# The start of an LSTM kernel: h0 @ Wh joins the product of x's first pair, the first step's cell is placed among the last operations of Wh's split, and the first pairs of x are waited for one by one

## The chip, the cores and the metric

The kernel runs on one core of one Trainium2 chip. A core has five engines, each of which works through its own queue in order: TensorE (PE; its weight loads are shown apart as PEld), VectorE (DVE), ScalarE (ACT), GpSimd (POOL) and SyncE (SP). They meet through semaphores. The metric is the device time of one execution in microseconds. Before the change three runs gave 2269.09, 2270.43 and 2270.66 us, median 2270.43.

## What is computed

An LSTM over 16 sequences of 512 steps, with 512 inputs and 512 hidden units, whose outputs are added to x:

```python
def ref(x, h0, Wx, Wh, b):            # x (16, 512, 512), h0 (16, 512)
    xW = jnp.einsum('ntd,dg->ntg', x, Wx) + b
    def step(carry, xw_t):
        prev_h, prev_c = carry
        a = xw_t + prev_h @ Wh        # (16, 2048): gates i, f, o, g
        i = sigmoid(a[:, :H]); f = sigmoid(a[:, H:2*H])
        o = sigmoid(a[:, 2*H:3*H]); g = tanh(a[:, 3*H:])
        next_c = f * prev_c + i * g
        next_h = o * tanh(next_c)
        return (next_h, next_c), next_h
    _, hs = lax.scan(step, (h0, zeros), swapaxes(xW, 0, 1))
    return x + swapaxes(hs, 0, 1)
```

Every step needs the h of the step before it; only the products with Wx are free of the recurrence.

## The kernel before, in words

**Layout.** Two steps form a pair of 32 rows (2 times 16 sequences); 8 pairs are loaded as one tile `xs`. Each of the four column groups of TensorE (32 output partitions each) takes one quarter of the hidden units, so a product is always four matmuls side by side. The hidden units are also cut into two halves, called a and b (0 and 1), so that one half's cell can be computed while the other half's products run.

**Products with Wx.** `turn_x(q)` (L173) transposes pair q of x on DVE into `xT`; ahead of it a small copy `seen` (L179) takes one column of each block, so that the wait for the DMAs of x is made once. `project(q, c)` (L185) multiplies quarter c of the inputs into a PSUM bank `xb[q % 4]` that already holds the bias, in fp32, as two matmul records for each matmul. `seed(t, h)` (L196) has ACT copy half h of the gates of step t from that bank to the bank `gates[h][t % 2]`, with the rows of the pair's other step set to zero by a mask.

**Products with Wh.** Wh is scaled and split into three fp16 parts, `wq[0]` to `wq[2]`. The split works on 8 pieces n = 0 to 7 of 128x1024 (quarter c = n // 2 of the rows, half of the gates). For each: q1 rounds the scaled weight to fp16 (L469 on ACT or L471 on DVE), r1 takes the rest (L474, DVE), q2 rounds that (L478, ACT), r2 takes the rest again (L481, DVE), and q3 rounds that (L483, ACT). The scales come from the largest magnitudes of Wh: `bound` (L430) reduces rows on DVE (L436) or on ACT (L434), and `scales(h)` (L444) makes the factors for half h of the rows with seven small DVE operations. `products(t, i, kh, h)` (L204) multiplies the parts of half kh of h by `wq[i-1]` into the gates of half h, eight matmuls each.

**Step 0** has no split h. `first_products` (L219) multiplies h0, transposed on DVE into `hT0` (L501), by Wh itself in fp32, straight into the banks `gates[h][0]`, after the seeds.

**A step's cell** is the list `STEP` (L24), executed by `act` (L270): turn and turno transpose the gates on DVE (L246), fold and foldo combine parts (L253), tanh, sig, sigo and scale are ACT's (L280 to L288), mix and cell DVE's (L290, L296), ctanh ACT's (L298), p1 writes the first fp16 part of the new h (L306), h the fp32 one (L300), copy (L310), p2 (L312), rem (L316) and p2r (L320) the others. Half a's products can start with p1_a; the others need p2, copy and p2r.

**TensorE's order in a step** is the list `STEP_PE` (L23): twelve products, named by part, half of h and half of the gates, and then two quarters (x0, x1) of a product with Wx for a pair that comes two pairs later. The first of a step is q3aa.

**What sets the order.** All five queues are filled in the order in which the program issues (the scheduling is by hand). The start does this: DMAs of Wh, Wx and most of x on SP's queue, of h0 and of the first three pairs of x on POOL's (`load_first`, L156, 8 DMAs a pair); bias into the four xb banks (L418); then a loop over the 8 pieces (L493) that issues the split's operations one piece behind the other. In its third round (n == 2) it issues `turn_x` for three pairs, `hT0`, and the products with Wx for pairs 0 and 1; in its sixth (n == 5) the seeds of steps 0 and 1. After the loop the step loop begins with t = 0: its first products, x0 and x1 for pair 2, and its cell.

DMAs on a queue share a small set of semaphores. An engine waits for each semaphore by itself, so that a copy that needs eight DMAs has several waits ahead of it.

Of the kernel before, what the change touches and what calls it, by code (L numbers as in the profile page):

```python
# [7 lines left out]
FP = mybir.dt.float32  # L8
# [3 lines left out]
ALU = mybir.AluOpType  # L12
PSUM = bass.MemoryType.PSUM

P = 128
Q = 32
XB = 16
LO = 4096.0
# [6 lines left out]
    "turn_a turno_a fold_a tanh_a foldo_a sig_a turn_b sigo_a scale_a mix_a fold_b "  # L25
    "tanh_b cell_a ctanh_a turno_b foldo_b sig_b p1_a sigo_b h_a copy_a mix_b p2_a "
    "scale_b cell_b rem_a ctanh_b p2r_a p1_b h_b copy_b p2_b rem_b p2r_b"
)


@with_exitstack
def lstm_residual(ctx: ExitStack, tc: tile.TileContext, x, h0, wx, wh, b, out):
# [28 lines left out]
    nc = tc.nc  # L61
    N, T, D = x.shape
    H = h0.shape[1]
# [37 lines left out]
    wq = [const.tile([P, NK, G * H], HP, tag=f"wq{i}", name=f"wq{i}") for i in range(3)]  # L101

    wx_j = wx_sb.rearrange("p k (g c j u) -> p k j g c u", g=G, c=NK, j=NJ)
    wh_j = wh_sb.rearrange(
        "p k (e g h c j u) -> p k e h j g c u", e=2, g=2, h=2, c=2, j=NJ
    )
    wq_j = [
        w.rearrange("p k (g h c j u) -> p k h j g c u", g=G, h=2, c=2, j=NJ) for w in wq
    ]
    bias = const.tile([P, G * P], FP, tag="bias", name="bias")  # L110
    mask = const.tile([P, S2], FP, tag="mask", name="mask")
    zero = const.tile([1, G * P], HP, tag="zero", name="zero")
    amax = const.tile([P, 5], FP, tag="amax", name="amax")
    top = const.tile([P, 2], FP, tag="top", name="top")
    bits = const.tile([P, 2, 2], FP, tag="bits", name="bits")
    sc = const.tile([P, 2, 4], FP, tag="sc", name="sc")
# [55 lines left out]

    def turn_x(q):  # L173
        s, i = divmod(q, XP)
        if i == 0 or q == FIRST:

            a, e = (0, FIRST) if q == 0 else (i, XP)
            seen = tmp.tile([P, XP, NK], FP, tag="seen", name=f"seen_{q}")
            nc.vector.tensor_copy(  # L179
                seen[:, a:e], xs[s].rearrange("p i (c u) -> p i c u", c=NK)[:, a:e, :, 0]  # L180
            )
        xT[q] = xtp.tile([P, NK, Q], FP, tag="xT", name=f"xT_{q}")
        nc.vector.transpose(xT[q].rearrange("p c m -> p (c m)"), xs[s][:, i])  # L183

    def project(q, c):  # L185
        for j in range(NJ):
            nc.tensor.matmul(  # L187
                xb[q % NXB][j * Q : (j + 1) * Q],
                lhsT=xT[q][:, c],
                rhs=wx_j[:, c, j],  # L190
                start=False,
                stop=False,
                skip_group_check=True,
            )

    def seed(t, h):  # L196
        nc.scalar.mul(  # L197
            gates[h][t % 2][:, :GU].rearrange("p (g u) -> p g u", g=G),
            xb[t // 2 % NXB].rearrange("p (g h u) -> p h g u", g=G, h=2)[:, h],
            mask[:, t % 2 : t % 2 + 1],  # L200
        )
# [14 lines left out]
                    skip_group_check=True,  # L216
                )

    def first_products(kh, h, hT):  # L219
        for cc in range(2):  # L220
            for e in range(2):
                for j in range(NJ):
                    nc.tensor.matmul(
                        gates[h][0][j * Q : (j + 1) * Q, (1 - e) * P : (2 - e) * P],
                        lhsT=hT[:, 2 * kh + cc],
                        rhs=wh_j[:, 2 * kh + cc, e, h, j],
                        start=False,
                        stop=False,
                        skip_group_check=True,
                    )  # L230


    gc = [state.tile([P, 2, 2 * N], FP, tag=f"gc{h}", name=f"gc{h}_init") for h in range(2)]
# [118 lines left out]
    def residual(p):  # L352
        s, i = divmod(p, XP)
        if i == 0:
            ob[s] = outp.tile([P, XP, P], FP, tag="ob", name=f"ob_{s}")
        hb = work.tile([P, P], FP, tag="hb", name=f"hb_{p}")
        nc.vector.transpose(hb, hs[p].rearrange("p c m -> p (c m)"))  # L357
        add = nc.vector if p == NP - 1 else nc.gpsimd
        add.tensor_tensor(ob[s][:, i], hb, xs[s][:, i], ALU.add)  # L359
        if p == NP - 1:  # L360
            put_pair(s, i, [nc.sync, nc.scalar])
        elif s == NS - 1:
            put_pair(s, i, [nc.sync])
        elif i == XP - 1:
            put(s)
# [8 lines left out]
    for c in range(NK):  # L374
        for e in range(2):
            f = slice(e * GH, (e + 1) * GH)
            nc.sync.dma_start(out=wh_sb[:, c, f], in_=wh[c * P : (c + 1) * P, f])
    nc.vector.memset(zero, 0.0)
    nc.vector.memset(h_in, 0.0)
    nc.vector.memset(ones, 1.0)  # L380
    for j in range(NJ):
# [45 lines left out]
                )  # L427
    nc.scalar.copy(bias, xb[0])

    def bound(i, c, on_act, f=slice(0, G * H)):  # L430
        w = wh_sb[:, c, f]
        if on_act:
            junk = tmp.tile([P, G * H], HP, tag="junk", name=f"junk_{i}", bufs=1)
            nc.scalar.activation(junk[:, f], w, AF.Abs, accum_out=amax[:, i : i + 1])  # L434
        else:
            nc.vector.tensor_reduce(  # L436
                amax[:, i : i + 1],
                w,
                mybir.AxisListType.X,
                ALU.max,  # L440
                apply_absolute_value=True,
            )

    def scales(h):  # L444


        nc.vector.tensor_reduce(
            top[:, h : h + 1], amax[:, 3 * h : 3 + 2 * h], mybir.AxisListType.X, ALU.max
        )
        t = top[:, h : h + 1].bitcast(I32)  # L450
        e, inv = bits[:, h, 0:1], bits[:, h, 1:2]
        nc.vector.tensor_scalar(
            inv.bitcast(I32), t, EXP, EXP, ALU.bitwise_and, ALU.bitwise_xor
        )
        nc.vector.tensor_scalar(e.bitcast(I32), t, EXP, None, ALU.bitwise_and)
        nc.vector.tensor_scalar(RS2[h], inv, 2.0**12, 0.5, ALU.mult, ALU.min)
        nc.vector.tensor_scalar(RS[h], inv, 2.0**13, 1.0, ALU.mult, ALU.min)
        nc.vector.tensor_scalar(S[h], e, 2.0**-14, 1.0, ALU.mult, ALU.max)
        nc.vector.tensor_scalar(RSL[h], RS[h], 1.0 / LO, None, ALU.mult)

    r1, r2 = {}, {}

    def split(n, k):

        c, e = divmod(n, 2)
        w = wh_sb[:, c, e * GH : (e + 1) * GH]
        f = [q[:, c, (1 - e) * GH : (2 - e) * GH] for q in wq]
        if k == 0 and n < 6:
            nc.scalar.mul(f[0], w, RS2[c // 2])  # L469
        elif k == 0:  # L470
            nc.vector.tensor_scalar(f[0], w, RS2[c // 2], None, ALU.mult)  # L471
        elif k == 1:
            r1[n] = tmp.tile([P, GH], FP, tag="r1", name=f"r1_{n}")
            nc.vector.scalar_tensor_tensor(  # L474
                r1[n], w, RS[c // 2], f[0], ALU.mult, ALU.subtract
            )
        elif k == 2:
            nc.scalar.copy(f[1], r1[n])  # L478
        elif k == 3:
            r2[n] = tmp.tile([P, GH], FP, tag="r2", name=f"r2_{n}")  # L480
            nc.vector.tensor_tensor(r2[n], r1[n], f[1], ALU.subtract)  # L481
        else:
            nc.scalar.mul(f[2], r2[n], LO)  # L483

    NH = 2 * NK
    bound(0, 0, False)
    bound(1, 1, True, slice(0, GH))
    bound(2, 1, False, slice(GH, 2 * GH))
    scales(0)
    split(0, 0)  # L490
    split(0, 1)
    split(1, 0)
    for n in range(NH):  # L493
        if n == 1:
            bound(3, 2, False)
            bound(4, 3, True)
            scales(1)
        if n == 2:
            for q in range(FIRST):
                turn_x(q)  # L500
            nc.vector.transpose(hT0.rearrange("p c m -> p (c m)"), h_in)  # L501
            for q in range(2):
                for c in range(NK):
                    project(q, c)
        if n + 1 < NH:
            split(n + 1, 1)
        split(n, 2)
        split(n, 3)
        if n:
            split(n - 1, 4)  # L510
        if n + 2 < NH:
            split(n + 2, 0)
        if n == 5:
            for t in range(2):
                for h in range(2):
                    seed(t, h)
    split(NH - 1, 4)

    for t in range(T):
        s, ti = divmod(t, XB)  # L520
        q, half = divmod(t + 4, 2)
        if ti == 0:
            hist[s] = outp.tile([P, XP, NK, Q], FP, tag="hist", name=f"hist_{s}")

        for op in STEP_PE.split():
            if op[0] == "x":
                if q < NP:
                    project(q, 2 * half + int(op[1:]))
            elif t:
                products(t, int(op[1]), "ab".index(op[2]), "ab".index(op[3]))  # L530
            elif op[1] == "3":
                first_products("ab".index(op[2]), "ab".index(op[3]), hT0)

        for op in STEP.split():
            name, h = op.split("_")
            act(t, name, "ab".index(h))

        if t + 2 < T:
            seed(t + 2, 0)
        if t % 2:  # L540
            for h in range(2):
                unscale(t // 2, h)
            if q + 1 < NP:
                turn_x(q + 1)
        else:
            if t and q + 1 < NP:
                put_bias(q + 1)
            if t:
                residual(t // 2 - 1)
        if t + 2 < T:  # L550
            seed(t + 2, 1)
        if ti == 0 and s + 2 < NS:
            load_xs(s + 2)
# [29 lines left out]
```

## Time and profile before

| | |
|---|---|
| profiled execution, us | 2270.51 |
| its span, first to last instruction, us | 2268.2 |
| median of three runs, us | 2270.43 |
| PE busy | 2234.5 us (99%), 57444 matmul records |
| DVE busy | 1957.2 us (86%) |
| ACT busy | 1839.7 us (81%) |
| products with Wh (L210) | 49056 records, 1427.4 us |
| products with Wx (L187) | 8192 records, 966.7 us |
| first product of step 1 starts (timeline) | 44.78 us |

How to read it: the span runs from the first to the last instruction; the time of the execution has some 2.3 us around that. The mean duration of a matmul record is longer than its share of the engine, since four run side by side. Busy shares over the whole span tell of the 512 steps; the start, some 2% of the span, has to be read in the timeline, in order of time.

### The profile page before, as it was taken

The page shows a single profiled execution, that of the slowest core. Times are in us where ns is not written, and L with a number is a line of the kernel's source. Part 1 is how long each engine was busy: PE and PEld are TensorE (multiplying, and loading weights), DVE is VectorE, ACT ScalarE, POOL GpSimd, SP SyncE. Part 2 cuts the span into 40 slices and gives each one's busy share as a digit, 9 for nine tenths or more (in the row PEclk, how much of TensorE's full clock was granted, in tenths as well). Part 3 has the DMA queues.
Part 4 walks back from the last instruction along what each step waited for, and adds up shares of the span by engine and source line. Part 5 has one row for each costly group of instructions (what it writes and reads, how often), then busy time and mean ns, then how long its engine had stood idle before and what let it go on. Part 6 is the DMA issues. An engine that isn't in the chain of part 4 may idle for free.

```text
span 2268.2 us, 138001 instructions
## 1 busy us (share of the span) xinstructions
PE 2234.5 (99%) x57444; PEld 1466.8 (65%) x57444; DVE 1957.2 (86%) x11853; ACT 1839.7 (81%) x7959; POOL 131.1 (6%) x287
## 2 busy tenths in 40 slices
PE   6999999999999999999999999999999999999997
PEld 3666666666666666666666666666666666666665
DVE  7888888888888888888888888888888888888887
ACT  6888888888888888888888888888888888888887
POOL 2000000000000000000000000000000000000000
PEclk9999999999999999999999999999999999999999
DMA  5011111111111111111111111111111111111001
GB/s 166 16 22 23 16 17 16 22 22 19 17 17 19 22 22 16 17 17 22 23 18 16 17 20 23 22 16 17 16 23 22 19 16 17 20 22 21 15 9 17
DMA packets 297716, 50.93 MB, mean 22 GB/s; under 512 B 294593, under 2 KB 295041, under 8 KB 297089
## 3 DMA queue, kind: packets, MB, share of 16 engines
q1 hardware_dynamic: 295872, 41.85, 11.4%
q8 instruction: 450, 7.37, 1.4%
q14 instruction: 176, 1.44, 0.2%
q0 software_dynamic: 896, 0.23, 0.1%
q10 hardware_dynamic: 322, 0.04, 0.0%
HBM read 25.21 MB, written 16.78 MB: 19 GB/s over the span
## 4 chain that ended last, share of the span: by engine, by line
PE 97%; DMA 1%; DVE 1%; issue 0%; ACT 0%; POOL 0%; SPq 0%; POOLq 0%; DVEq 0%
PE gates L210 59%; PE xb L187 38%; DMA xs<-in_x_dram 1%; DVE r L481 0%; DMA h_in<-in_cond_dram 0%; DVE r L474 0%; ACT wq L483 0%; SPq L347 0%; POOL h_in L382 0%; DMA out_dram<-ob 0%; DVE wq L471 0%; DVE xT L183 0%; POOLq L578 0%; DVE pr L290 0%; POOL ob L359 0%
## 5 line engine op out<-in xcount | busy, mean ns | idle before, releaser
L210 PEld LDWEIGHTS <-parts 128*32 128x32 f16 x49056 | 1224.7, 96 | 442.2 <-DVE parts L306 306.0
L210 PE MATMUL gates<-wq,parts 128*32 128x256 f16 x49056 | 1427.4, 273 | 7.0 <-DVE parts L306 7.0
L187 PE MATMUL xb<-wx_sb,xT 128*32 128x512 f32 x8192 | 966.7, 593 | 17.4 <-DMA xs<-in_x_dram 17.4
L246 DVE STREAM_TRANSPOSE gt<-gates 128x192 f32<-128x192 f32 x1024 | 392.0, 383 | 216.2 <-PE gates L210 168.1
L187 PEld LDWEIGHTS xb<-wx_sb,xT 128*32 128x32 f32 x8192 | 235.4, 110 | 344.1 <-issue 340.3
L197 ACT ACTIVATE gates<-xb,mask 128x256 f32<-128x256 f32 x1024 | 451.3, 441 | 0.0
L280 ACT ACTIVATE gc<-pre 128x32 f32<-128x32 f32 x1022 | 234.6, 230 | 259.7 <-DVE pre L253 248.3
L288 ACT ACTIVATE os<-so,sc 128x32 f32<-128x32 f32 x1024 | 329.6, 322 | 16.7
L310 ACT COPY parts<-parts 128x32 f16<-128x32 f16 x1022 | 214.3, 210 | 132.2 <-DVE parts L306 132.2
L253 DVE SCALAR_TENSOR_TENSOR pre<-gt 128x96 f32<-128x96 f32 x1024 | 255.1, 249 | 0.0
L282 ACT ACTIVATE sif<-pre 128x64 f32<-128x64 f32 x1024 | 244.9, 239 | 0.0
L359 POOL TENSOR_TENSOR ob<-hb,xs 128x128 f32<-128x128 f32 x255 | 116.5, 457 | 2121.6 <-DVE hb L357 2039.4
L246 DVE STREAM_TRANSPOSE gto<-gates 128x64 f32<-128x64 f32 x1024 | 231.2, 226 | 0.0
L286 ACT ACTIVATE so<-preo 128x32 f32<-128x32 f32 x1024 | 227.0, 222 | 0.0
L298 ACT ACTIVATE tch<-gc 128x32 f32<-128x32 f32 x1024 | 226.8, 221 | 0.1
L320 DVE SCALAR_TENSOR_TENSOR parts<-rem,parts 128x32 f16<-128x32 f32 x1022 | 195.9, 192 | 35.5
L253 DVE SCALAR_TENSOR_TENSOR preo<-gto 128x32 f32<-128x32 f32 x1024 | 193.6, 189 | 17.5
L312 DVE SCALAR_TENSOR_TENSOR parts<-parts,hist 128x32 f16<-128x32 f16 x1022 | 193.3, 189 | 17.7
L290 DVE TENSOR_TENSOR pr<-sif,gc 128x64 f32<-128x64 f32 x1022 | 205.8, 201 | 0.0
L306 DVE TENSOR_TENSOR parts<-os,tch 128x32 f16<-128x32 f32 x1022 | 196.9, 193 | 0.0
L296 DVE TENSOR_TENSOR gc<-pr 128x32 f32<-128x32 f32 x1024 | 193.3, 189 | 0.0
L300 DVE SCALAR_TENSOR_TENSOR hist<-os,tch 128x32 f32<-128x32 f32 x1024 | 190.2, 186 | 0.3 <-ACT tch L298 0.3
(49 smaller groups left out, 740.1 us busy)
## 6 DMA issues: line engine op xcount, KB each, us to landing
xs<-in_x_dram SPq DMA_DIRECT2D x992, 16.0 KB, 2.1
out_dram<-ob SPq DMA_DIRECT2D x992, 16.0 KB, 1.6
wh_sb<-in_L_cond_Wh_dram SPq DMA_DIRECT2D x8, 512.0 KB, 7.8
wx_sb<-in_L_cond_Wx_dram SPq DMA_DIRECT2D x8, 512.0 KB, 11.7
out_dram<-ob SPq DMA_DIRECT2D x60, 8.0 KB, 1.5
xs<-in_x_dram SPq DMA_DIRECT2D x32, 10.0 KB, 2.3
xs<-in_x_dram POOLq DMA_DIRECT2D x24, 8.0 KB, 5.2
h_in<-in_cond_dram POOLq DMA_DIRECT2D x4, 8.0 KB, 6.0
```

Of the source, the lines that this page charges most:

```text
L187: nc.tensor.matmul(xb[q % NXB][j * Q : (j + 1) * Q], lhsT=xT[q][:, c], rhs=wx_j[:, c, j], start=False, stop=False, skip_group_check=True,)
L197: nc.scalar.mul(gates[h][t % 2][:, :GU].rearrange("p (g u) -> p g u", g=G), xb[t // 2 % NXB].rearrange("p (g h u) -> p h g u", g=G, h=2)[: ...
L210: nc.tensor.matmul(g[j * Q : (j + 1) * Q, :GU], lhsT=a[:, cc, k * N : (k + 2) * N], rhs=wq_j[i - 1][:, 2 * kh + cc, h, j], start=False, st ...
L246: nc.vector.transpose(gt.rearrange("p b m -> p (b m)"), gates[h][t % 2][:, b0 * Q : b1 * Q])
L253: nc.vector.scalar_tensor_tensor(pre.rearrange("p g (c n) -> p (g c) n", c=2), gt[:, :, (1 - t % 2) * N : (2 - t % 2) * N], 1.0 / LO, gt[: ...
L280: nc.scalar.activation(gc[h][:, 0], v["pre", h][:, 0], AF.Tanh)
L282: nc.scalar.activation(new("sif", t, h, [P, 2, 2 * N]), v["pre", h][:, 1:3], AF.Sigmoid)
L286: nc.scalar.activation(new("so", t, h, [P, 2 * N]), v["preo", h][:, 0], AF.Sigmoid)
L288: nc.scalar.mul(new("os", t, h, [P, 2 * N]), v["so", h], S[h])
L290: nc.vector.tensor_tensor(new("pr", t, h, [P, 2, 2 * N]), v["sif", h], gc[h], ALU.mult)
L298: nc.scalar.activation(new("tch", t, h, [P, 2 * N]), gc[h][:, 1], AF.Tanh)
L310: nc.scalar.copy(slots(t, h, 2), slots(t, h, 0))
```

## The change

All of it lies ahead of step 1; the step loop then runs from t = 1.

- The order of the start is now one written list, `START`, which the function `start` executes. It names every bound (`b.0.v`: quarter 0 on DVE; `.s`: on ACT; `1a`, `1b`: a quarter's two halves), scale (`S.0`), operation of the split (`q1.2.v`: q1 of piece 2 on DVE), pair of x (`xT.0`), product (`H.c`, `P.q.c`), seed and operation of step 0's cell. So pieces are taken in the order 2, 0, 3, 1, 5, 7, 6, 4, five of the roundings are DVE's (q1.0, q1.2, q2.2, q3.3, q3.7; before, q1.6 and q1.7 were), and step 0's cell stands between the last operations of the split.
- `H.c` multiplies quarter c of h0 by Wh into `xb[0]`, ahead of the products with Wx of pair 0. Since h0's rows in `hT0` are those of the pair's first step, the seed carries the sum into step 0's gates. The matmuls have 256 columns instead of 128, and there are half as many. `first_products` into the gates is gone.
- `turn_x` makes its small copy for each of the pairs 0, 1 and 2 by itself.
- `Z` adds twelve matmuls of zeros, one partition deep and 512 columns wide, to the bank `xb[3]`, after the first half of pair 2's product.
- The bounds have eight places (a memset of `amax` is new); r1 has four buffers instead of three. The load of the third `xs` tile is issued at the same place in SP's queue.

```diff
+START = (
+    "b.0.v hT H.0 b.1a.v b.1b.v H.1 S.0 q1.2.v q1.3.s H.2 q1.0.v q1.1.s r1.2 b.2.s r1.0 "
+    "H.3 r1.3 b.3a.s b.3b.s q2.2.v xT.0 q2.3.s r1.1 P.0.0 q2.0.s r2.2 q2.1.s S.1 q3.2.s "
+    "r2.0 P.0.1 q1.5.s r2.3 q3.0.s r2.1 q1.7.s q3.3.v q3.1.s P.0.2 xT.1 q1.6.s r1.5 "
+    "q1.4.s P.0.3 r1.7 P.1.0 seed.0.0 r1.6 seed.0.1 P.1.1 seed.1.0 turn_a turno_a q2.7.s "
+    "turn_b xT.2 fold_a q2.6.s fold_b P.1.2 foldo_a r1.4 tanh_a sig_a sigo_a scale_a "
+    "tanh_b sig_b P.1.3 P.2.0 P.2.1 turno_b r2.6 q2.4.s q2.5.s mix_a mix_b cell_a foldo_b "
+    "Z r2.4 ctanh_a q3.6.s cell_b p1_a h_a q3.4.s r2.5 sigo_b ctanh_b scale_b seed.1.1 "
+    "copy_a p2_a rem_a r2.7 q3.5.s p1_b h_b p2r_a copy_b q3.7.v p2_b rem_b p2r_b seed.2.0 "
+    "seed.2.1"
+)
...
-    wh_j = wh_sb.rearrange(
-        "p k (e g h c j u) -> p k e h j g c u", e=2, g=2, h=2, c=2, j=NJ
-    )
+    wh_j = wh_sb.rearrange("p k (e g c j u) -> p k e j g c u", e=2, g=2, c=NK, j=NJ)
...
-        if i == 0 or q == FIRST:
-            a, e = (0, FIRST) if q == 0 else (i, XP)
+        if i == 0 or q <= FIRST:
+            a, e = (i, i + 1 if q < FIRST else XP)
             seen = tmp.tile([P, XP, NK], FP, tag="seen", name=f"seen_{q}")
...
-    def first_products(kh, h, hT):
-        for cc in range(2):
-            for e in range(2):
-                for j in range(NJ):
-                    nc.tensor.matmul(
-                        gates[h][0][j * Q : (j + 1) * Q, (1 - e) * P : (2 - e) * P],
-                        lhsT=hT[:, 2 * kh + cc],
-                        rhs=wh_j[:, 2 * kh + cc, e, h, j],
...
+    def first_products(c):
+        for e in range(2):
+            for j in range(NJ):
+                nc.tensor.matmul(
+                    xb[0][j * Q : (j + 1) * Q, (1 - e) * GU : (2 - e) * GU],
+                    lhsT=hT0[:, c],
+                    rhs=wh_j[:, c, e, j],
...
-            r1[n] = tmp.tile([P, GH], FP, tag="r1", name=f"r1_{n}")
+            r1[n] = tmp.tile([P, GH], FP, tag="r1", name=f"r1_{n}", bufs=4)
...
+    def start(op, a="", b=""):
+        if op == "b":
+            bound(a, b == "s")
+        elif op == "S":
+            scales(int(a))
+        elif op == "hT":
             nc.vector.transpose(hT0.rearrange("p c m -> p (c m)"), h_in)
...
+        elif op == "xT":
+            turn_x(int(a))
+        elif op == "H":
+            first_products(int(a))
+        elif op == "P":
+            project(int(a), int(b))
+        elif op == "Z":
+            for _ in range(12):
+                zeros(xb[NXB - 1], False)
+        elif op == "seed":
+            seed(int(a), int(b))
+        elif "_" in op:
+            name, h = op.split("_")
+            act(0, name, "ab".index(h))
+        else:
+            split(op, int(a), b == "s")
+
+    hist[0] = outp.tile([P, XP, NK, Q], FP, tag="hist", name="hist_0")
+    for op in START.split():
+        start(*op.split("."))
+    load_xs(2)
+
+    for t in range(1, T):
...
-            elif t:
+            else:
                 products(t, int(op[1]), "ab".index(op[2]), "ab".index(op[3]))
-            elif op[1] == "3":
-                first_products("ab".index(op[2]), "ab".index(op[3]), hT0)
```

## The prediction

> **What bounds the kernel now.** I read the page first, then the timeline of the first 60 us, then the chain of waits there, then busy time in stretches cut where the granted TensorE clock changes.
>
> The page: 511 of the 512 steps are TensorE work.
>
> ```profile
> span 2268.2 us, 138001 instructions
> PE 97%; DMA 1%; DVE 1%; issue 0%; ACT 0%; POOL 0%; SPq 0%; POOLq 0%; DVEq 0%
> PE gates L210 59%; PE xb L187 38%; DMA xs<-in_x_dram 1%; DVE r L481 0%; DMA h_in<-in_cond_dram 0%; DVE r L474 0%; ACT wq L483 0%; SPq L347 0%; POOL h_in L382 0%; DMA out_dram<-ob 0%; DVE wq L471 0%; DVE xT L183 0%; POOLq L578 0%; DVE pr L290 0%; POOL ob L359 0%
> ```
>
> The chain is all TensorE, in the products with Wh's parts (L210) and with Wx (L187). The code of steps 1 to 511 is not edited, and from step 2 on TensorE has no gap (434.00 us busy in 1000 to 1434). So the change is worth what it moves one point: the end of step 1's TensorE work. The timeline of that region (start, duration, engine, line, what, in brackets the idle time before it and what ended it):
>
> ```profile
> 26.96 0.17 DVE L179 COPY seen<-xs 128x12 f32<-128x12 f32 x1 [4.30 <-DMA xs<-in_x_dram]
> ...
> 36.54 3.70 PE L223 MATMUL gates<-wh_sb,hT 128*32 128x128 f32 x128 [0.57 <-ACT gates L197]
> ...
> 42.26 0.38 DVE L246 STREAM_TRANSPOSE gt<-gates 128x192 f32<-128x192 f32 x1
> ...
> 44.53 0.19 DVE L306 TENSOR_TENSOR parts<-os,tch 128x32 f16<-128x32 f32 x1
> ...
> 44.78 4.10 PE L210 MATMUL gates<-wq,parts 128*32 128x256 f16 x96 [2.83 <-DVE parts L306]
> ...
> 48.71 1.89 PE L187 MATMUL xb<-wx_sb,xT 128*32 128x512 f32 x16
> ...
> 50.43 2.79 PE L210 MATMUL gates<-wq,parts 128*32 128x256 f16 x96
> ```
>
> DVE stands still 4.30 us until all three pairs of x have landed, then works without a pause; step 0's cell (from 42.26) waits behind the whole split; TensorE waits for the cell's first product p1 (44.53). Step 1's TensorE work runs to **50.60** (the chain of waits has L210 again from there). Its 96 products take 4.10 us where step 2's take 2.62 (chain), and the stretches say why (columns: stretch, length, busy time of five engines, granted clock, DMA):
>
> ```profile
> 37.24:40.66 3.42, 3.42 (x120) 3.08 (x112) 3.38 (x4) 2.88 (x4) 0.00 (x0) 1.00 0.17 25
> 40.66:44.07 3.41, 1.29 (x13) 0.13 (x4) 3.00 (x10) 3.15 (x7) 0.00 (x0) 1.00 0.16 24
> 44.07:47.48 3.41, 2.70 (x52) 2.10 (x56) 2.12 (x16) 2.31 (x11) 0.00 (x0) 0.50 0.22 33
> 47.48:50.60 3.12, 3.12 (x76) 1.75 (x68) 2.41 (x15) 1.77 (x10) 0.00 (x0) 1.00 0.16 26
> ```
>
> After 3.41 us with TensorE 38% busy the clock is halved; after one with 79% it is whole again. Step 1 pays 4.10 - 2.62 = 1.48 us for it.
>
> **The change, part by part.**
>
> *Waits by pair.* The chain of waits gives when the last DMA of each pair lands: 10.09 + 5.86 = 15.95, 16.23 + 4.97 = 21.20, 21.48 + 5.21 = 26.69. The instruction of `turn_x` stands in DVE's queue ahead of all later splitting and of the cell. With the new order below DVE reaches pair 0 at 19.2, pair 1 at 26.9, pair 2 at 31.7: 3.2, 5.7 and 5.0 us after landing. The 4.30 us go. Price: two more copies of 0.17 us and two more sets of waits (0.27 us from last landing to copy, in the chain), some 0.7 us of DVE.
>
> *h0 @ Wh into the bank of pair 0.* Out: 128 matmul records, 3.70 us, between P.1 and P.2. In: 64 records of 256 columns. Row L187 (512 columns, whole clock) is 1.72/16 = 0.107 us each, so 256 columns are 0.053, 64 of them 3.4 us, at half clock 6.8. They run from 10.3 to 16.4 as Wh's quarters land (last 15.54), when TensorE had no work; Wx's quarters land at 19.40, 22.09, 25.21 and 27.13 by the DMA landings, so P.0.3 ends at 28.9 anyway. Cost nothing; without that cover, under 2 us, since seeds aren't asked for before 29.6. The first cell then needs the seeds alone.
>
> *Bounds and scales.* hT moves ahead in DVE's queue and waits for h0 (lands 9.81; start 10.0), and both bounds of quarter 1 are now DVE's (one was ACT's). The scale is ready at 13.4 instead of 12.45. This 0.9 us is inside the DVE sum.
>
> *The DVE sum* (start to next start in a full queue). From 10.0: hT 0.2; two bounds 2.3; two scale sets 1.6; q1.2, q1.0, q2.2, q3.3, q3.7 at 0.67 = 3.35 (L471 takes 0.75; q2.2 as a DVE copy has no row, between that and ACT's 1.03: I take 0.75, the same size and types); eight r1 at 1.20 = 9.6; eight r2 at 1.14 = 9.1; three turns of x 1.8; 22 cell operations, 1.5 a half = 3.0 (timeline 42.26 to 46.33 less its stalls). Sum 30.95: the last cell operation, p2r_b, ends at **40.9**, against 46.14 + 0.19 = 46.33 now. Replaying the old order in this way gives p1_a within 0.1 us of its measured start, so I trust the terms.
>
> *ACT beside it.* From 13.4: six q1 at 1.06, bounds 4.2, seven q2 at 0.95, six q3 at 0.97, six seeds 0.37, the cell 2.0: 27.3, so 40.7. It is as full as DVE; the latest thing TensorE needs from it, q3.5, ends at 39.8, 0.7 before DVE's own q3.7 (40.5). That is its slack.
>
> *Step 1 on TensorE.* p1_a comes at 36.8, seed.1.1 (behind scale_b on ACT) at 38.7, so the first products trickle; q3ba needs q3.7 (40.5), q2ba needs p2r_b (40.9). From 40.9 there remain q2ba, q2bb, q1bb, q2ab, q3bb: five twelfths of 2.62 = 1.09, and x0, x1 1.72. At whole clock the end is **43.7**. The next cell's p1_a, 2.2 us after q2ba's end as at 48.06 to 50.22 now, comes at 43.4 and delays nothing.
>
> *Z, the twelve zero matmuls.* Queued behind P.2.1 (ends near 34.8), ahead of step 1's products: 12 x 512 columns, 2.6 us at whole clock, 5.1 at half. They end at 37.4, at worst near 39.1 with a late clock; products have slack until about 39.8. Cost nothing. [...] Where the edges fall I can't know; I take the middle, **44.6**.
>
> [...]
>
> **Sum:** 50.60 - 44.6 = 6.0 us (5.1 to 6.9). The profiled execution took 2270.51, so 2264.5; it lies 0.08 above the median of the three runs: **2264.4**.
>
> **Rivals.**
> 1. *Forecast, 0.82:* DVE's sum sets the start; 2263.5 to 2265.3 from the clock alone. 0.2% of the time, what can be told from no change, is 4.5 us, so the gain is only a little beyond that.
> 2. *Hand-offs eat it, 0.11:* the new order lets ACT and DVE wait for each other at q1/r1 and q2/r2. Now DVE shows one such wait of 0.97 us; three more, or the 2.4 of pair 2, make 2264.4 + 2.7 = 2267.1. For: ACT's sum equals DVE's. Against: in the new order each r1 or r2 stands one or two operations behind its input.
> 3. *The waits by pair don't do what they say, 0.03:* if pair 0's copy waits for all three (26.69), DVE stands still from 19.2 to 26.9, 7.7 us: 2271.9 after the 0.2 that the later waits save. Against: the old copy waited for 26.69, not for the rest of the same tile (lands 42.5), so waits go by the slice read.
> [...]
>
> Chances: faster by over 0.2% 0.78 (most of 1, a little of 2), within 0.17, slower 0.05. Range 2262.8 to 2267.4: the clock's ends, 0.8 of spread between runs, and rival 2. [...]
>
> **What would show it.** `seen` three times, none with a long wait for xs; L223 gone, 64 records on xb before 17; p2r_b's end near 40.9; a granted clock below 1 somewhere in 37 to 45; L210 of step 2 from 44.6. Wrong if DVE waits more than 1 us in all after 10.3, if ACT's q3.5 ends after 40.5, or if the steps from 2 on change their 4.34 us.

## The result and the profile after

Eight runs of the changed kernel give a median of **2264.30 us** (2262.51 to 2265.43), eight of the kernel before 2270.38 (2269.09 to 2272.09): 6.1 us less, a ratio of 0.9972 with a 95% interval of 0.9961 to 0.9983. The forecast was 2264.4.

The profiled execution took 2265.43 us, the slowest of the eight; its span is 4.6 us shorter than before. Its page, the span and the chain of waits by engine and by line (lines have new numbers: L223 are the products with Wh's parts, L200 those with Wx):

```profile
span 2263.6 us, 137913 instructions
...
PE 98%; DMA 1%; issue 0%; SPq 0%; DVE 0%; POOLq 0%; POOL 0%
PE gates L223 59%; PE xb L200 39%; DMA wx_sb<-in_L_cond_Wx_dram 1%; DMA wh_sb<-in_L_cond_Wh_dram 0%; SPq L389 0%; PE xb L420 0%; SPq L359 0%; DMA out_dram<-ob 0%; DMA xs<-in_x_dram 0%; POOLq L590 0%; POOL ob L371 0%; DVE parts L332 0%; DVE gt L258 0%; DVE ob L371 0%; DVE parts L324 0%
```

The split's lines on DVE (L474 and L481 before) are gone from the chain. What stands ahead of TensorE is now the load of Wx, ahead of that the load of Wh. The timeline of the start (start, duration, engine, line, what, and in brackets the idle time before it with what ended it):

```profile
10.53 4.10 PE L235 MATMUL xb<-wh_sb,hT 128*32 128x256 f32 x48 [0.43 <-issue]
...
18.90 0.18 DVE L192 COPY seen<-xs 128x4 f32<-128x4 f32 x1
...
26.20 0.17 DVE L192 COPY seen<-xs 128x4 f32<-128x4 f32 x1
...
27.88 9.08 PE L200 MATMUL xb<-wx_sb,xT 128*32 128x512 f32 x56 [0.87 <-DMA xs<-in_x_dram]
...
30.37 0.38 DVE L258 STREAM_TRANSPOSE gt<-gates 128x192 f32<-128x192 f32 x1 [0.23 <-ACT gates L210]
...
31.10 0.17 DVE L192 COPY seen<-xs 128x4 f32<-128x4 f32 x1
...
36.19 0.18 DVE L318 TENSOR_TENSOR parts<-os,tch 128x32 f16<-128x32 f32 x1
...
36.89 2.76 PE L420 MATMUL xb<-zero 1*128 1x512 f16 x12
...
39.58 4.46 PE L223 MATMUL gates<-wq,parts 128*32 128x256 f16 x96
...
40.10 0.19 DVE L332 SCALAR_TENSOR_TENSOR parts<-rem,parts 128x32 f16<-128x32 f32 x1
...
43.81 1.95 PE L200 MATMUL xb<-wx_sb,xT 128*32 128x512 f32 x16
```

None of the three copies of x shows an idle time of note: the 4.30 us are gone. h0 @ Wh (L235) runs from 10.53, the cell's first transpose starts at 30.37 where it started at 42.26, its p1_a ends at 36.37 where it ended at 44.72. But the products of step 1 do not start there. The chain in order of time (start, duration, what):

```profile
27.88 9.08 PE xb L200 x56
36.96 2.69 PE xb L420 x12
39.65 4.39 PE gates L223 x96
44.04 1.73 PE xb L200 x16
45.77 2.64 PE gates L223 x96
```

TensorE has no gap from 27.88 on, when Wx's last quarter has landed (the profile puts this wait down to x, whose pair 0 had long been turned; in the other execution of this kernel, below, to Wx). In this execution its own queue, with the zeros in it, is what step 1 starts behind, 3.2 us after p1_a. Step 1's TensorE work ends at 45.77, against 50.60. The stretches, cut where the clock changes, say why its queue is so long (stretch, length, busy time of PE, PEld, DVE, ACT and POOL, granted clock, DMA):

```profile
26.88:30.29 3.41, 2.54 (x16) 0.59 (x16) 3.26 (x3) 3.07 (x5) 0.00 (x0) 0.50 0.11 19
30.29:33.70 3.41, 3.41 (x20) 0.79 (x16) 3.33 (x11) 3.38 (x10) 0.00 (x0) 0.50 0.14 22
33.70:37.12 3.42, 3.42 (x33) 0.83 (x26) 3.31 (x10) 3.42 (x8) 0.00 (x0) 1.00 0.14 21
37.12:40.53 3.41, 3.41 (x48) 1.86 (x50) 3.13 (x11) 3.41 (x10) 0.00 (x0) 1.00 0.14 23
40.53:43.94 3.41, 3.41 (x73) 2.76 (x68) 0.78 (x4) 0.88 (x5) 0.00 (x0) 0.50 0.20 30
```

The clock is halved until 33.70, and again from 40.53, although TensorE is shown busy for the whole stretch before that. All of that stretch up to 39.65 is the zeros. (The granted clock is on record only from its first change on; ahead of that the column stands at 1.00 whatever the clock is. In the kernel before it reads 1.00 from 27.45 to 30.42, and there a matmul of L187 took 2.96 / 16 = 0.185 us, against 0.107 later.) So two questions were open: which part of the change brings the 6 us, and whether the start is now bound by TensorE or by DVE and ScalarE.

From the start of step 2's products to the end the trace of before has 2217.8 us left, and that of after 2218.0; the steps are untouched.

### The profile page after: what moved, and what is told of

It is laid out like the page before. It is cut to its first block, busy times and chain, and to the rows that moved or that the text cites. A ratio compares the mean times of both kernels' runs of the same rounds, so it can differ in the third digit from the quotient of the medians.

```text
span 2263.6 us, 137913 instructions
## 1 busy us (share of the span) xinstructions
PE 2243.6 (99%) x57392; PEld 1511.3 (67%) x57392; DVE 1955.8 (86%) x11859; ACT 1834.9 (81%) x7958; POOL 131.5 (6%) x287
## 4 chain that ended last, share of the span: by engine, by line
PE 98%; DMA 1%; issue 0%; SPq 0%; DVE 0%; POOLq 0%; POOL 0%
PE gates L223 59%; PE xb L200 39%; DMA wx_sb<-in_L_cond_Wx_dram 1%; DMA wh_sb<-in_L_cond_Wh_dram 0%; SPq L389 0%; PE xb L420 0%; SPq L359 0%; DMA out_dram<-ob 0%; DMA xs<-in_x_dram 0%; POOLq L590 0%; POOL ob L371 0%; DVE parts L332 0%; DVE gt L258 0%; DVE ob L371 0%; DVE parts L324 0%
## 5 line engine op out<-in xcount | busy, mean ns | idle before, releaser
L223 PEld LDWEIGHTS <-parts 128*32 128x32 f16 x49056 | 1263.4, 96 | 400.5 <-DVE parts L318 300.7
L223 PE MATMUL gates<-wq,parts 128*32 128x256 f16 x49056 | 1429.7, 273 | 4.2 <-DVE parts L318 4.2
L200 PE MATMUL xb<-wx_sb,xT 128*32 128x512 f32 x8192 | 972.5, 595 | 5.4 <-DMA wx_sb<-in_L_cond_Wx_dram 4.5
L200 PEld LDWEIGHTS xb<-wx_sb,xT 128*32 128x32 f32 x8192 | 240.8, 110 | 331.3 <-issue 324.3
L210 ACT ACTIVATE gates<-xb,mask 128x256 f32<-128x256 f32 x1024 | 449.9, 440 | 0.3 <-PE xb L200 0.3
```

Of the source, the lines that this page charges most:

```text
L200: nc.tensor.matmul(xb[q % NXB][j * Q : (j + 1) * Q], lhsT=xT[q][:, c], rhs=wx_j[:, c, j], start=False, stop=False, skip_group_check=True,)
L210: nc.scalar.mul(gates[h][t % 2][:, :GU].rearrange("p (g u) -> p g u", g=G), xb[t // 2 % NXB].rearrange("p (g h u) -> p h g u", g=G, h=2)[: ...
L223: nc.tensor.matmul(g[j * Q : (j + 1) * Q, :GU], lhsT=a[:, cc, k * N : (k + 2) * N], rhs=wq_j[i - 1][:, 2 * kh + cc, h, j], start=False, st ...
```

## The experiments

Three theories were set against each other. **A**: TensorE is now the bound, and one-partition matmuls count as idle for its clock. **B**, the prediction's: the work of DVE (and ScalarE) sets where step 1's work ends. **C**: any busy TensorE holds the clock. Three sets of four kernels ran, each set on another chip, beside the kernel before (medians 2269.62, 2270.15 and 2270.36). The intervals of the ratios are some 0.2% wide, 4 to 5 us, so a single microsecond is read from medians together with the trace. Only the first set has the changed kernel on its own chip; in the other two its 2264.30 and 2264.08 come from other chips. What the traces allow across chips: from step 2's first product to the end they have 2217.8 to 2218.0 us left, in the changed kernel and in all variants but two (h0 behind the seeds 2218.5, waits by pair alone 2218.8).

**The changed kernel again.**

> The changed kernel as it is, beside the others on one chip. All theories: 2264.3 us, give or take 0.6. Its trace: TensorE without a gap from the landing of Wx's last quarter (27.8 to 27.9) to the end of step 1, the clock halved for some 3.4 us somewhere between 37 and 45, end of step 1's TensorE work between 44.0 and 45.8.

2264.08 us, ratio 0.9975 (0.9966 to 0.9985). Its trace ends step 1 at 44.41, 1.36 earlier than the other profiled execution, though p1_a and p2r_b end only 0.28 earlier. The rest is the clock, granted at 31.36 here and at 33.70 there: the 56 products with Wx took 8.06 us against 9.08. TensorE's timeline, and the two stretches around the zeros, which by the chain run from 35.66 to 38.38:

```profile
35.59 2.79 PE L420 MATMUL xb<-zero 1*128 1x512 f16 x12
38.31 4.39 PE L223 MATMUL gates<-wq,parts 128*32 128x256 f16 x96
...
44.25 2.83 PE L223 MATMUL gates<-wq,parts 128*32 128x256 f16 x96
```
```profile
34.78:38.19 3.41, 3.41 (x24) 1.04 (x12) 3.41 (x8) 3.41 (x8) 0.00 (x0) 1.00 0.10 14
38.19:41.60 3.41, 3.41 (x65) 2.44 (x68) 1.78 (x8) 2.13 (x6) 0.00 (x0) 0.50 0.16 25
```

The first stretch is busy throughout, three quarters of it (2.5 of 3.41 us) with the zeros, and the clock is halved at its end.

**No zeros.**

```diff
-    "Z r2.4 ctanh_a q3.6.s ...
+    "r2.4 ctanh_a q3.6.s ...
```

> Without the twelve zero matmuls. Theory A (TensorE is now the bound of the start, and one-partition matmuls count as idle for the clock): the products of step 1 start as soon as half a is ready, near 38.7 at the latest, instead of behind the zeros, the clock is halved as before: 0.3 to 0.9 us faster than the changed kernel, 2263.4 to 2264.0. Theory B (the DVE sum sets the start, the zeros hide beside it): no difference, 2264.3. Theory C (any busy TensorE holds the clock, so the zeros do what a filler should): the clock falls earlier and step 1 runs at half clock throughout, 0.5 to 1.5 slower, 2264.8 to 2265.8.

2264.27 us, ratio 0.9976 (0.9967 to 0.9985): no difference to 2264.08, theory B's figure; the 0.3 to 0.9 us that A expected did not come. The clock is halved without the zeros too:

```profile
33.72:37.13 3.41, 0.89 (x16) 0.22 (x9) 3.35 (x10) 3.41 (x6) 0.00 (x0) 1.00 0.15 22
37.13:40.54 3.41, 2.03 (x40) 1.72 (x43) 2.90 (x11) 3.24 (x10) 0.00 (x0) 0.50 0.12 19
40.54:43.96 3.42, 3.42 (x60) 2.41 (x55) 1.23 (x7) 0.82 (x4) 0.00 (x0) 0.50 0.19 28
```

26% busy without the zeros, 100% with them, and halved after both: C falls, since a busy TensorE with the zeros did not hold the clock. The half clock lasts longer here, 6.8 us against 3.4 in both traces of the changed kernel, and step 1 ends at 45.46 by the chain. But this execution took 2265.00, one of the slower ones; by the medians the zeros neither gain nor cost anything.

**A filler that is 128 partitions deep**, with real data into columns that nothing reads, and with weights of zero:

```diff
-            for _ in range(12):
-                zeros(xb[NXB - 1], False)
+            for _ in range(24):
+                nc.tensor.matmul(gates[0][0][:, GU:], lhsT=wq[0][:, 1, GH : GH + P],
+                                 rhs=wq[0][:, 1, GH : GH + GU], start=False, stop=False,
+                                 skip_group_check=True)
```
```diff
+    deep = const.tile([P, P], HP, tag="deep", name="deep")
+    nc.vector.memset(deep, 0.0)
...
+            for _ in range(12):
+                nc.tensor.matmul(xb[NXB - 1], lhsT=deep,
+                                 rhs=wq[0][:, 1, GH : GH + G * P], start=False, stop=False,
+                                 skip_group_check=True)
```

> Instead of the zeros 24 matmuls of the same time in all (2.6 us at whole clock), 128 partitions deep, with parts of Wh as both operands, into columns of a gates bank that nothing reads. Theory A (the clock counts how much of the array works): the clock stays whole through step 1, whose 96 products take under 3.2 us instead of 4.4; 1.2 to 1.7 us faster than the changed kernel, 2262.6 to 2263.1. Theory C (busy time alone counts): as the changed kernel, 2264.3.

> Instead of the zeros twelve matmuls of the same 512 columns, 128 partitions deep, moving parts of Wh against weights that are all zero. If the depth is what counts, like the run with real data: 2262.6 to 2263.1 and a whole clock through step 1. If what counts is that values change in the array, like the zeros: 2264.3 and a halved clock.

2263.02 us (ratio 0.9972, 0.9960 to 0.9983) and 2263.18 (0.9970, 0.9959 to 0.9982), about 1 us faster than the changed kernel beside them: a little less than the 1.2 to 1.7 that A asked for, in its direction. The stretches and the timeline of the filler with zero weights, which runs from 34.81:

```profile
35.97:39.38 3.41, 2.65 (x44) 1.38 (x46) 3.41 (x12) 3.41 (x8) 0.00 (x0) 1.00 0.16 25
39.38:42.79 3.41, 3.27 (x87) 1.88 (x80) 2.63 (x14) 2.34 (x11) 0.00 (x0) 1.00 0.15 22
```
```profile
37.50 0.40 PE L223 MATMUL gates<-wq,parts 128*32 128x256 f16 x8
38.67 2.91 PE L223 MATMUL gates<-wq,parts 128*32 128x256 f16 x88 [0.76 <-ACT gates L210]
...
43.12 2.83 PE L223 MATMUL gates<-wq,parts 128*32 128x256 f16 x96
```

78% busy with deep work and the clock stays; the last 88 matmuls take 2.91 us where 96 took 4.39. Weights of zero hold it as real ones do (2.91 us with either). That it is the depth fits the 64 bias matmuls of the kernel before, one partition with real values, which in 7.05 us did not raise the clock (0.110 us each, see below). But the deep fillers also move real data where `Z` moves zeros; a deep filler that moves zeros was not run, so the two are not told apart for holding the clock. And now TensorE waits, for a seed (L210) in ScalarE's queue, and then for the copy of half b behind it (`copy_b`, ends at 39.82): with a whole clock it isn't the bound any more.

**One copy for all three pairs again.**

```diff
-        if i == 0 or q <= FIRST:
-            a, e = (i, i + 1 if q < FIRST else XP)
+        if i == 0 or q == FIRST:
+            a, e = (0, FIRST) if q == 0 else (i, XP)
```

> The changed kernel, but one copy waits for all three pairs of x again, at the place of pair 0 in the order. Theory A (the wait sets DVE's queue, and DVE and ScalarE together set the start): DVE stands still from 19.0 until the third pair lands (26.7 to 27.7), everything behind it is 7.7 to 8.7 later; since TensorE has 1 to 2 us of slack against that, 6 to 8 us more than the changed kernel, 2270.2 to 2272.2, so the whole gain is gone. Rival (the written order is what brings the gain, the wait is covered by other work): under 2 us more, 2264.2 to 2266.2.

2271.88 us, ratio 1.0008 (0.9999 to 1.0018), inside theory A's range. The timeline shows the wait at the place of pair 0:

```profile
26.42 0.17 DVE L192 COPY seen<-xs 128x12 f32<-128x12 f32 x1 [7.86 <-DMA xs<-in_x_dram]
```

The whole gain is gone: the written order with one joint wait at the place of pair 0 is worth nothing. A joint wait further back in the order was not tried.

**The waits by pair alone**, in the kernel before:

> The kernel before, with the waits by pair as its only edit: the three copies and transposes still stand in a row in DVE's queue ahead of the rest of the split. Theory A: no gain, since DVE still can't pass the third pair; TensorE's first product starts earlier, nothing else: within 1 us of the kernel before. Rival (waiting by pair is a gain by itself): 2 us or more faster than before.

2268.99 us, ratio 0.9995 (0.9986 to 1.0005), 1.2 below the median beside it (1 was allowed), and the interval holds no change at all. DVE still waits 3.2 us once for x. p1_a ends 1.2 earlier than in the kernel before (43.54 against 44.72); 0.8 of that is the third pair's copy, at 26.17 instead of 26.96. The trace holds a side effect: the products with Wx start at 22.80 instead of 27.45, h0's product takes 5.37 us instead of 3.70, and step 1's 96 products 2.92 instead of 4.10, so that the half clock fell elsewhere:

```profile
43.60 2.92 PE L210 MATMUL gates<-wq,parts 128*32 128x256 f16 x96 [1.17 <-DVE parts L306]
```

So the waits by pair bring 1 us or so by themselves, not clear of noise, and the order as written needs them.

**The cell behind the split**, in the old order of `STEP`, everything else as in the changed kernel:

> The changed kernel, but the operations of step 0's cell stand behind the whole split, in the old order. Theory A (DVE's and ScalarE's work is the same in sum, only its end changes): split done near 37.3, the first product p1 of half a near 39.6 instead of 36.4, p2r of half b near 41.3 instead of 40.3; 0.5 to 1.5 us more, 2264.7 to 2265.7. Rival (the place of the cell is what brings most of the gain): 3 to 5 us more, 2267.2 to 2269.2.

2266.48 us, ratio 0.9984 (0.9975 to 0.9994): 2.2 more than the changed kernel's 2264.30, between the two ranges, so neither is right. The trace shows what was left out:

```profile
33.26 4.63 DVE L501 TENSOR_TENSOR r<-r,wq 128x1024 f32<-128x1024 f32 x4 [1.63 <-ACT wq L498]
```

Without the cell's operations DVE gets ahead of ScalarE's roundings and stands still for 1.63 us. The cell among the split also fills that. p1_a ends at 40.64 and not near 39.6, p2r_b at 42.25 and not 41.3. In this execution step 1's 96 products also take 4.83 us, where step 2's take 2.79, which fits a halved clock; what the stall and the clock cost each was not taken apart.

**h0 @ Wh into the gates again**, with `first_products` as before the change, behind step 0's seeds:

```diff
-    "... P.0.3 r1.7 P.1.0 seed.0.0 r1.6 seed.0.1 P.1.1 ...
+    "... P.0.3 r1.7 seed.0.0 r1.6 seed.0.1 H.0.0 H.0.1 H.1.0 H.1.1 P.1.0 P.1.1 ...
```

> The changed kernel, but h0 @ Wh goes straight into the gates again, behind the seeds of step 0 on TensorE's queue and ahead of the product of pair 1. Theory A (the product joined to pair 0 costs nothing because it runs while Wx is on its way; behind the seeds it stands between them and the cell): L223's old 128 records run from about 31 to 36, the first transpose of the gates starts near 35.8 instead of 30.4, and DVE waits there with half the split behind it; 3.5 to 4.5 us more, 2267.7 to 2268.7. Rival (TensorE has room, no effect): 2264.2.

2268.94 us, ratio 0.9995 (0.9986 to 1.0005), at the upper end of A's range. The timeline:

```profile
30.38 4.11 PE L238 MATMUL gates<-wh_sb,hT 128*32 128x128 f32 x128 [0.57 <-ACT gates L212]
...
33.77 0.38 DVE L261 STREAM_TRANSPOSE gt<-gates 128x192 f32<-128x192 f32 x1 [3.72 <-PE gates L238]
```

DVE waits 3.72 us for the product and p1_a ends at 40.11. This execution's mean granted clock was 0.999, against 0.995 in the changed kernel's, its step 1's products took 3.09 us against 4.46, and it took 2267.18, the fastest of its ten; in it h0's product took 4.1 us where the expectation had 5.

**One operation more on DVE**, an r2 done twice, in the changed kernel and in that with the deep zeros; **one more on ScalarE**, a q3 done twice, in the latter:

```diff
+            for _ in range(2 if n == 5 else 1):
                 nc.vector.tensor_tensor(r2[n], r1[n], f[1], ALU.subtract)
```
```diff
+            for _ in range(2 if n == 4 else 1):
                 cast(on_act, f[2], r2[n], LO)
```

> The changed kernel with one operation of the split done twice on DVE (r2 of piece 5, 1.14 us more in the part between p1_a and p2_a; the second has the same result). Theory B, the prediction's step (DVE's sum sets where step 1's work ends): 0.9 to 1.1 us slower than the changed kernel, 2265.0 to 2265.2. Theory A (TensorE itself, at half clock in step 1, ends last, and DVE has slack): 0 to 0.4 slower, 2264.1 to 2264.5.

> The same doubled operation, in the kernel with the 128-partition filler, where step 1 runs at whole clock (2263.2). Theory A (with a whole clock TensorE waits for the last cell operations, so their end is the start's bound): 0.8 to 1.1 us slower, 2264.0 to 2264.3. Rival (TensorE's own queue is the bound there too): no effect, 2263.2.

> In the kernel with the 128-partition filler one operation of the split done twice on ScalarE instead (q3 of piece 4, 0.95 us more, ahead of seed.1.1 and both copies). If ScalarE is as much the bound as DVE (the chain of waits of that kernel runs through ScalarE's queue): 0.7 to 1.0 us slower, 2263.9 to 2264.2. If it has the 0.7 us of slack that the prediction gave it: 0.2 to 0.3 slower.

In the changed kernel: 2265.45 us, ratio 0.9979 (0.9971 to 0.9988), 1.2 to 1.4 above its two medians, nearer to B's 0.9 to 1.1 than to A's 0.4 at most. The chips differ: measured against the kernel before on each chip it is 0.6 to 1.2, so A isn't excluded. The trace doesn't settle it: in this execution, the slowest of its eleven, the products with Wx start at 28.66 instead of 27.60 to 27.88 and the operations before the doubled one are already 1 us late. TensorE waits 0.19 us, by the profile for copy_b, and then has 64 records left at half clock (3.61 us, where with the deep zeros and the same dose 64 take 2.22):

```profile
41.46 3.61 PE L223 MATMUL gates<-wq,parts 128*32 128x256 f16 x64 [0.19 <-ACT parts L322]
```

With the deep zeros: 2264.05 (ratio 0.9973, 0.9963 to 0.9983) and 2263.91 (0.9974, 0.9963 to 0.9984), 0.87 and 0.73 above 2263.18. That median is of another chip, where the kernel before was 0.74 faster too, so the traces have to carry it, and here they agree. One 1.14 more on DVE moves p2r_b from 40.21 to 41.37 and step 2's start from 43.12 to 44.24; 0.95 more on ScalarE moves copy_b from 39.81 to 40.65 and step 2's start to 43.96. First DVE's, then ScalarE's:

```profile
40.48 2.22 PE L223 MATMUL gates<-wq,parts 128*32 128x256 f16 x64 [1.01 <-ACT parts L322]
...
41.17 0.19 DVE L332 SCALAR_TENSOR_TENSOR parts<-rem,parts 128x32 f16<-128x32 f32 x1
...
44.24 2.83 PE L223 MATMUL gates<-wq,parts 128*32 128x256 f16 x96
```
```profile
39.51 2.91 PE L223 MATMUL gates<-wq,parts 128*32 128x256 f16 x88 [1.48 <-ACT gates L210]
...
43.96 2.83 PE L223 MATMUL gates<-wq,parts 128*32 128x256 f16 x96
```

At a whole clock both engines bound the start, and neither has slack to speak of. The changed kernel as it is looks different in its two traces. The first product that needs p2r_b is q2ba, the eighth of step 1, and it starts at 41.68 and 41.27, 1.4 and 1.3 us after p2r_b has ended (40.29 and 40.01). q3.7 ends 1.0 and 0.8 us ahead of the sixth, q3ba, which needs it. So there TensorE itself is the bound, by its late start and the half clock. By that a dose of 1.14 on DVE should have cost 0.2 to 0.3 us, as A said, and by the medians it cost 0.6 to 1.4. How it reaches the end at half clock stays open.

**Deep fillers ahead of 27.8 too**; `F.9` is nine of those with weights of zero.

```diff
-    "... H.2 q1.0.v ... H.3 r1.3 ... P.0.0 q2.0.s ... P.0.1 q1.5.s ... P.0.2 xT.1 ...
+    "... H.2 F.2 q1.0.v ... H.3 F.9 r1.3 ... P.0.0 F.7 q2.0.s ... P.0.1 F.7 q1.5.s ... P.0.2 F.7 xT.1 ...
```

> The kernel with the 128-partition filler, and such fillers (2, 9, 7, 7, 7 matmuls) also in TensorE's gaps ahead of 27.8, so that the products with Wx run at whole clock. Theory A (what TensorE does ahead of 36 is covered by DVE and ScalarE): within 0.4 us of the kernel with one filler, 2262.8 to 2263.4, the granted clock whole from about 15 on. Rival (the half clock ahead of 31 still costs): 0.6 to 1.2 faster, 2262.0 to 2262.6.

2262.38 us (2262.08 to 2263.30), ratio 0.9967 (0.9955 to 0.9980): the fastest median of all, in the rival's range. None of its products from 19.97 on is at half clock: eights of records with Wx take 1.06 to 1.07 us where two of the changed kernel's take 1.93 and 1.94, 56 take 6.21 where it has 9.08, and the mean granted clock was 0.999 against 0.995. But its trace doesn't show the rival's reason:

```profile
37.16 0.40 PE L223 MATMUL gates<-wq,parts 128*32 128x256 f16 x8
38.31 2.91 PE L223 MATMUL gates<-wq,parts 128*32 128x256 f16 x88 [0.74 <-ACT gates L210]
```

TensorE waits for the same seed for as long as with one filler (0.74 and 0.76 us), and step 2 starts 0.36 earlier just as copy_b ends 0.36 earlier. That it keeps TensorE from being late in executions where the clock comes late, as in the one of the changed kernel above, would explain the median; it was not shown. Against the changed kernel it is 1.7 to 1.9 us by medians, on different chips.

The new order of the eight pieces and the roundings that moved between the engines were not tested alone. They are in the kernel with the cell behind the split, which is still 3.7 us faster than the one before.

## Why the prediction was right

The place was right: what moved is the end of step 1's TensorE work, and all else kept its 2218 us. So were the parts of the change that it named; taking out the waits by pair, the joined product or the place of the cell loses 7.6, 4.6 and 2.2 us by medians. What it named as the bound, DVE's sum, was right only in part.

*The waits.* DVE reaches the three copies at 18.90, 26.20 and 31.10 (said: 19.2, 26.9, 31.7). Rival 3, that a copy waits for all pairs, did not come about; the joint copy measured its price, 2271.88 where it said 2271.9.

*The DVE sum.* p2r_b ends at 40.29, said 40.9. The three turns of x took 0.3 us each in place of 0.6, 0.9 less in all; a start 0.1 later and a wait of 0.23 for a seed took some of it back. p1_a 36.37 (36.8), q3.7 39.86 (40.5), seed.1.1 38.69 (38.7), q3.5 39.78 (39.8).

*h0's product* cost nothing, as said, and is worth 4.6 us by medians (2268.94 - 2264.30) against the form behind the seeds.

*TensorE's own queue* is the step that was mis-sized. P.2.1 was to end near 34.8 and the zeros at 37.4, at worst 39.1; in the profiled execution they end at 36.96 and 39.65, in the other at 35.66 and 38.38. Wx's last quarter was used from 27.88 and 27.60 on, not from 27.13. And 34.8 comes out only if the clock is granted near 30.4, where it was in the kernel before (30.41). It was granted at 33.70 and 31.36: the stretch ahead of 30.29 had TensorE 74% busy (2.54 of 3.41 us), and the clock stayed halved behind it. That put step 1's end at 45.77, just past the 45.5 that the sum's 5.1 us stand for, in the slowest run, and at 44.41 in a run of median speed. No run shows the sum's own term, 44.6, an estimate halfway between 45.5 and the 43.7 of a whole clock: in these two executions the clock was halved for 3.41 us, from 40.53 and from 38.19.

So the sum "p2r_b, then five products and x0, x1" is not what these two executions ran through: DVE was 1.3 to 1.4 us ahead of q2ba. It is what the kernel with a whole clock runs through, with ScalarE's copy_b as close a bound: by the chain step 1 ends there at 43.29, 3.08 us after p2r_b, and with the dose on DVE at 44.41, 3.04 after it, where the sum had 2.81. Part of the agreement of the total is luck: DVE's end came 0.6 earlier and TensorE's start later than said.

*The zeros* cost nothing, as said (2264.27 without them), and the clock was halved after them. In the kernel before, matmuls of one partition had not raised it either:

```profile
3.00 7.05 PE L418 MATMUL xb<-brow,ones 1*32 1x256 f32 x64
```

These 64 of the bias ran back to back at 0.110 us each, where 256 columns at whole clock are 0.053 (half of the 0.107 that 512 took). That reading rests on the 0.110 us, since the column of the clock says nothing that early. The zeros bear it out: they took 0.60 to 0.63 us each at the start of the changed kernel (four, at 1.2 to 2.4 us) and 0.37 to 0.38 as `Z`, with the clock whole.

*Pair 2's 2.4 us*, which rival 2 and with it the range take in, are shown by no run: two of GpSimd's issues of x took 0.37 and 0.51 us longer than the rest (see below), and pair 2 had landed 3.4 us before DVE asked for it. *ScalarE's slack* of 0.7 us isn't there: q3.5 ends 0.08 before q3.7, which DVE had finished earlier than said, and once the clock is whole 0.95 more on ScalarE moved step 2 by 0.84.

Runs of the changed kernel spread over 2.6 to 2.9 us, those with a deep filler over 0.5 to 2.0. That the places at which the clock changes make the difference fits the traces; each trace is one execution, so it isn't shown.

## What to carry to other kernels

A wait for several transfers in one instruction holds up what stands behind it on that engine's queue: here the joint copy kept DVE still for 7.86 us and cost 7.6. Taking it apart gained little (1.2 us by medians, not clear of noise) until the order put work between the pieces. A first step that needs half of what the rest needs can be laid among the last preparation, and each side fills the other's stalls (here 2.2 us, with one stall of 1.63 on DVE). Before one calls an engine the bound because the chain runs through it, one more operation on its neighbours shows whether they have slack: here the chain named TensorE alone, and 1.14 us more on DVE still cost 0.6 to 1.4 by the medians, where the trace had let one expect slack.

## What the runs showed of the hardware

**What held the clock in these runs.** Twelve matmuls of zeros, one partition deep, filled a stretch of 3.41 us for three quarters and the clock was halved behind it (100% busy shown), as it was without them (26%). Matmuls of 128 partitions for the same time held it (78% busy shown with weights of zero), real weights as those of zero, both with real moving data: the last 88 products of step 1 took 2.91 us in both, where the changed kernel's 96 took 4.39 and 4.46. The clock was not granted after stretches at half speed that were 60% (2.03 of 3.41, the kernel without zeros) and 74% (2.54 of 3.41, the changed kernel) busy with deep work, and was granted after 79% (2.70 of 3.41, the kernel before).

**GpSimd's issues of DMAs beside DVE's roundings.** POOL's issue of a DMA of x takes 0.51 us. In the changed kernel two of 24 take longer, 0.88 and 1.02, both beside a DVE operation from fp32 to fp16 of 0.69 to 0.75 us (a third, begun 0.30 us before such an operation, took 0.51). The second in POOL's timeline and DVE's:

```profile
18.09 1.02 POOL L175 DMA_DIRECT2D xs<-in_x_dram  x1
```
```profile
18.30 0.69 DVE L498 CAST wq<-r 128x1024 f16<-128x1024 f32 x1
```

DVE's operation ends at 18.99, POOL's issue 0.12 later; the other ends 0.11 after DVE's. The two took 0.37 and 0.51 us longer than the rest. That DVE's operation is what held them fits these times; no run tested it. The kernel before has none of it: its two such operations start at 34.81 and 37.93, behind the last issue (21.48), and no issue of x takes above 0.53 us. Pair 2 landed at 27.73 instead of 26.69, 3.4 us before DVE asked for it.
